# Moving parts of the second layer's vector work to GpSimd, TensorE and ScalarE in a four-layer kernel

## The chip, the cores and the metric

The kernel runs on one core of a Trainium2 chip. The metric is the device time of one execution in microseconds (us). Three runs of the kernel before took 3173.59, 3174.82 and 3178.38 us; the median is 3174.82 us.

A core has engines that work side by side, each through its own queue in order: TensorE (PE in the profile, its weight loads PEld), VectorE (DVE), ScalarE (ACT), GpSimd (POOL) and SyncE (SP), which here issues DMAs. An instruction waits for others through semaphores; while it waits, what stands behind it on its engine waits too. SBUF and PSUM are the two memories on the chip; matrix products land in PSUM.

## The reference

Four layers follow each other on x of 4 x 1024 tokens by 128 features. Each layer normalises x, makes an attention-like part s and a feed-forward part g, and adds s * silu(g) to x. The change concerns the second layer (L1):

```
xn = layernorm(x)
# attention over the 16 heads of one token (8 features each), c = 32 groups of t = 128 tokens
q, k_, v = (xn * mask) @ Wq.T + bq, ... Wk ..., ... Wv ...
scores = einsum('cthd,ctgd->cthg', q, k_) * scale      # 16 x 16 for each token
attn = entmax15(scores, axis=-1)                       # sorts each row of 16
s = einsum('cthg,ctgd->cthd', attn, v)

# feed-forward: 8 experts, the best 2 of each token, weighted
logits = x @ router_w
combine = softmax of the two largest logits, 0 elsewhere
gate = silu(einsum('th,ehf->etf', x, w1)); up = einsum('th,ehf->etf', x, w3)
out = einsum('te,eth->th', combine, einsum('etf,efh->eth', gate * up, w2))
x = x + s * silu(out)
```

The kernel puts the weight of `combine` on the input of the up product instead of the output: up is linear in x, so (c x) W3 = c (x W3).

## The kernel before, in words

Tokens lie on the 128 partitions, in 32 tiles of 128 tokens by 128 features. The second layer works in eight units of four tiles. A unit has two parts, written as generators that yield between steps: `heads1` (the attention) and `moe1` (the experts).

`heads1` first makes q, k and v of each tile with two matrix products (L729, L730) into a PSUM tile `pq`; ScalarE copies k and v to `kv` in SBUF (L731, L732). `multiply` (L716) makes the scores of one tile: a product of 16 x 16 x 8 elements for each token (L720, 2048 elements, VectorE) and a sum over the last 8 (L724, VectorE). After all four tiles it yields "scores". Then come `sort16` (L675; L698 and L699 are the maximum and minimum of pairs on VectorE, L688 and L689 copies on ScalarE, in ten stages) and the entmax on 128 x 1024 elements (L746 to L780), which goes back and forth between GpSimd (L748, L758, L759, L766, L772, L776), VectorE (two scans L752 and L753, then L761, L762, L768, L770, L771, L774) and ScalarE. Last come, for each tile, the products of attention and values (L790, GpSimd, 16 x 8 x 16 elements) and their sum over the last 16 (`values`, L785, VectorE).

`moe1` makes the logits, finds the best two (`top2`, with L197 and L198 on GpSimd) and the weights `comb` (L818). `thirds` (L204) splits `comb` into three bf16 parts (five small VectorE operations, L209 to L213) and turns them so that the tokens lie along a row (L216). `shares` (L221) spreads the row of one expert over all partitions with a bf16 product (L224). For each expert VectorE multiplies the turned input `xnT` by that row, which gives `xin` (L832); TensorE makes `pg` from `xnT` (L837) and `pu` from `xin` (L839), twice for 256 columns; ScalarE takes the silu (L840), VectorE multiplies (L841), and `down` (L828) adds the result to `po`. The down product of an expert is issued after the next expert's first products.

`layer1` (L620) runs `weave` over the present unit's heads (20 steps) and experts (11 steps), the next unit's heads up to "scores" (`upto`, 4 steps), and pieces of the third layer's preparation (`beside`). `weave` takes the part that is least far, by its share of steps. After it `update` (L648) turns the experts' result, multiplies it into s (L652, VectorE) and adds it to x (L654, GpSimd). What `weave` writes is an order of priority: when the program is built, a scheduler of the framework orders the queue of each engine by it and by the times it expects, so an operation of the next unit can stand ahead of one of this unit. Pool `p1` has one buffer of a name and `p2` two. PSUM has 4 buffers "mm", 2 "tr" and 2 "o".

Of the kernel before, what the change touches and what calls it, by code (L numbers as in the profile page):

```python
# [10 lines left out]
F32 = mybir.dt.float32  # L11
# [4 lines left out]
ALU = mybir.AluOpType  # L16
AX = mybir.AxisListType
# [3 lines left out]
P = 128  # L21
# [3 lines left out]
D = 128  # L25
# [64 lines left out]
def drain(gen):  # L90
    for _ in gen:
        pass
# [235 lines left out]
HT = NT // 2  # L328
# [291 lines left out]
def layer1(k, W, x_all, eps5, ps, beside):  # L620

    nc, tc = k.nc, k.tc
    with tc.tile_pool(name="l1", bufs=1) as p1, tc.tile_pool(name="l1d", bufs=2) as p2:

        keep = p1.tile([P, HT * 256], F32, tag="keep", name="keep")
        nc.vector.memset(keep, 1.0)
        nc.vector.memset(keep.rearrange("p (r n) -> p r n", n=16)[:, :, 0:1], 0.0)
        units = [(half, b) for half in range(2) for b in range(NB)]

        def start(half, b):  # L630
            first = b * NT + half * HT
            x = x_all[:, first : first + HT, :]
            xn = p2.tile([P, HT, D], F32, tag="xn", name="xn")
            k.layernorm(p2, x, xn, eps5, HT)
            xnT = p2.tile([P, HT * P], F32, tag="xnT", name="xnT")
            k.transpose_tiles(ps, "tr", [xn[:, t, :] for t in range(HT)], xnT)
            maskedT = None
            if half == 0:

                masked = p2.tile([P, D], F32, tag="masked", name="masked")  # L640
                nc.gpsimd.tensor_tensor(masked, xn[:, 0, :], k.c("tril"), ALU.mult)
                maskedT = p2.tile([P, P], F32, tag="maskedT", name="maskedT")
                k.transpose_tiles(ps, "tr", [masked], maskedT)
            s = p2.tile([P, HT, D], F32, tag="s", name="s")
            gT = p2.tile([P, HT * P], F32, tag="gT", name="gT")
            return x, s, gT, heads1(k, W, p1, p2, ps, xnT, maskedT, s, keep), moe1(k, W, p2, ps, xnT, gT)

        def update(x, s, gT):  # L648

            k.transpose_tiles(  # L650
                ps, "tr", [gT[:, t * P : (t + 1) * P] for t in range(HT)], s.rearrange("p t d -> p (t d)"),
                lambda out, in_: nc.vector.tensor_tensor(out, out, in_, ALU.mult),  # L652
            )
            nc.gpsimd.tensor_tensor(x, x, s, ALU.add)  # L654

        def upto(heads):

            while next(heads) != "scores":
                yield

        now = start(*units[0])
        drain(upto(now[3]))
        for n in range(len(units)):
            x, s, gT, heads, moe = now
            parts = [(heads, 20), (moe, 11)]
            if n + 1 < len(units):
                now = start(*units[n + 1])
                parts.append((upto(now[3]), 4))
                parts.append((islice(beside, 2), 2))
            weave(*parts)  # L670
            update(x, s, gT)
        drain(beside)
# [34 lines left out]
def heads1(k, W, p1, p2, ps, xnT, maskedT, s, keep):  # L707

    nc = k.nc
    R = 4 * 16  # L710
    kv = p2.tile([P, 4, 2, P], F32, tag="kv", name="kv")
    score = p2.tile([P, 4, 16, 16], F32, tag="score", name="score")

    pqs = []

    def multiply(t):  # L716

        each = [P, 16, 16, 8]
        prod = p2.tile(each, F32, tag="prods", name="prod")
        nc.vector.tensor_tensor(  # L720
            prod, pqs[t][:, 0:P].rearrange("p (h d) -> p h d", d=8).unsqueeze(2).to_broadcast(each),
            kv[:, t, 0, :].rearrange("p (g d) -> p g d", d=8).unsqueeze(1).to_broadcast(each), ALU.mult,
        )
        nc.vector.tensor_reduce(score[:, t], prod, AX.X, ALU.add)  # L724

    for t in range(4):
        lhsT = maskedT if maskedT is not None and t == 0 else xnT[:, t * P : (t + 1) * P]
        pq = ps.tile([P, 512], F32, tag="mm", name="pq")
        nc.tensor.matmul(pq[:, 0:384], lhsT, W["bd"].rearrange("p n c -> p (n c)"), start=True, stop=False)  # L729
        nc.tensor.matmul(pq[:, 0:384], k.c("ones")[0:1, :], W["bias"][0:1].rearrange("p n h d -> p (n h d)"), start=False, stop=True)  # L730
        nc.scalar.copy(kv[:, t, 0, :], pq[:, P : 2 * P])  # L731
        nc.scalar.copy(kv[:, t, 1, :].rearrange("p (d g) -> p g d", d=8), pq[:, 2 * P : 3 * P].rearrange("p (g d) -> p g d", d=8))  # L732
        pqs.append(pq)
        if t == 0:
            continue
        multiply(t - 1)
        yield
    multiply(3)
    yield "scores"
    scf = score.rearrange("p t h g -> p (t h g)")  # L740
    rows = lambda a: a.rearrange("p (r n) -> p r n", n=16)
    wide = lambda a: a.unsqueeze(2).to_broadcast([P, R, 16])
    srt = yield from sort16(k, p2, scf, R)
    new = lambda name: (p2 if name == "rest" else p1).tile([P, R * 16], F32, tag=name, name=name)
    top = p2.tile([P, R], F32, tag="top", name="top")
    nc.scalar.copy(top, rows(srt)[:, :, 0])  # L746
    z, zz, cum, rest = new("z"), new("zz"), new("cum"), new("rest")
    nc.gpsimd.tensor_tensor(rows(z), rows(srt), wide(top), ALU.subtract)  # L748
    nc.scalar.activation(zz, z, AF.Square)

    nc.gpsimd.memset(rows(zz)[:, :, 0:1], -1.0)
    nc.vector.tensor_tensor_scan(cum, keep, z, 0.0, ALU.mult, ALU.add)  # L752
    nc.vector.tensor_tensor_scan(rest, keep, zz, 0.0, ALU.mult, ALU.subtract)  # L753
    yield

    kinv = k.c("kinv").unsqueeze(1).to_broadcast([P, R, 16])
    mean, t1 = zz, cum
    nc.gpsimd.tensor_tensor(rows(mean), rows(cum), kinv, ALU.mult)  # L758
    nc.gpsimd.tensor_tensor(rows(rest), rows(rest), kinv, ALU.mult)  # L759
    nc.scalar.activation(t1, mean, AF.Square)  # L760
    nc.vector.tensor_tensor(t1, t1, rest, ALU.add)  # L761
    nc.vector.tensor_scalar(t1, t1, 0.0, None, op0=ALU.max)  # L762
    nc.scalar.activation(t1, t1, AF.Sqrt)
    yield
    tau = mean
    nc.gpsimd.tensor_tensor(tau, mean, t1, ALU.subtract)  # L766

    nc.vector.tensor_tensor(t1, tau, z, ALU.is_le)  # L768
    size = p2.tile([P, R], F32, tag="size", name="size")
    nc.vector.tensor_reduce(size, rows(t1), AX.X, ALU.add)  # L770
    nc.vector.tensor_tensor(rows(t1), k.c("kidx").unsqueeze(1).to_broadcast([P, R, 16]), wide(size), ALU.is_equal)  # L771
    nc.gpsimd.tensor_tensor(t1, t1, tau, ALU.mult)  # L772
    yield
    nc.vector.tensor_reduce(size, rows(t1), AX.X, ALU.add)  # L774
    nc.vector.tensor_tensor(size, size, top, ALU.add)
    nc.gpsimd.tensor_tensor(rows(t1), rows(scf), wide(size), ALU.subtract)  # L776
    yield
    attn = rest
    nc.scalar.activation(attn, t1, AF.Relu)
    nc.scalar.activation(attn, attn, AF.Square)  # L780
    yield
    before = None

    def values(t, prod):
        nc.vector.tensor_reduce(s[:, t, :].rearrange("p (h d) -> p h d", d=8), prod, AX.X, ALU.add)  # L785

    for t in range(4):
        each = [P, 16, 8, 16]
        prod = p2.tile(each, F32, tag="prodv", name="prod")
        nc.gpsimd.tensor_tensor(  # L790
            prod, attn.rearrange("p (t h g) -> p t h g", t=4, g=16)[:, t].unsqueeze(2).to_broadcast(each),
            kv[:, t, 1, :].rearrange("p (d g) -> p d g", d=8).unsqueeze(1).to_broadcast(each), ALU.mult,
        )
        if t:
            values(t - 1, before)
        before = prod
        yield
    values(3, before)


def moe1(k, W, p2, ps, xnT, gT):
    nc = k.nc
    pl = ps.tile([P, 512], F32, tag="o", name="pl")
    for t in range(HT):
# [7 lines left out]
    comb = p2.tile([P, HT, 8], F32, tag="comb", name="comb")  # L812
# [4 lines left out]
    nc.vector.reciprocal(best, best)  # L817
    nc.vector.tensor_tensor(comb, comb, best.unsqueeze(2).to_broadcast([P, HT, 8]), ALU.mult)  # L818

    thirds = k.thirds(p2, ps, comb, "m1")  # L820
    yield
    po = ps.tile([P, 512], F32, tag="o", name="po")
    share = k.shares(ps, thirds, 0)
    before = None

    def down(e, h):
# [1 line left out]
            nc.tensor.matmul(po, W["w2"][:, e, c, :], h[:, c, :], start=(e == 0 and c == 0), stop=(e == 7 and c == 1))  # L828

    for e in range(8):  # L830
        xin = p2.tile([P, 512], F32, tag="xin", name="xin")
        nc.vector.tensor_tensor(xin, xnT, share, ALU.mult)  # L832
        share = k.shares(ps, thirds, e + 1) if e < 7 else None
        h = p2.tile([P, 2, 512], F32, tag="h", name="h")
        for c in range(2):
            pg = ps.tile([P, 512], F32, tag="mm", name="pg")
# [4 lines left out]
            nc.vector.tensor_tensor(h[:, c, :], h[:, c, :], pu, ALU.mult)  # L841
        if before is not None:
            down(e - 1, before)
        before = h
        yield
    down(7, before)
    nc.scalar.activation(gT, po, AF.Silu)
# [1414 lines left out]
```

## Time and profile before

| what | value |
|---|---|
| median of three runs | 3174.82 us |
| the profiled execution, its own time | 3175.99 us |
| its span in the profile | 3174.2 us |
| mean granted TensorE clock | 0.738 |
| the second layer, from its first statistics to its last update | 576.3 to 1274.0 us |
| VectorE busy from 560 to 1275 us | 572.2 us |
| TensorE busy there | 517.0 us |
| GpSimd busy there | 280.7 us |
| ScalarE busy there | 247.4 us |

Busy time is the time in which an engine has an instruction under way; it says nothing about whether that instruction was the one that others waited for. In the lines of the profile, an entry of the timeline reads: start in us, duration in us, engine, line of the kernel, operation, output <- inputs, shapes, count, and in brackets the idle time of the engine before it with what ended it. Neighbouring equal entries are merged, as x4 tells. An entry of a group reads: line, engine, operation, output <- inputs, shapes, count, then busy us and mean ns of one, then idle us before them and what ended it. A line of the table by stretch reads: stretch, its length, busy us and count of PE, PEld, DVE, ACT and POOL, the granted TensorE clock as a share of full speed, the DMA share and GB/s.

### The profile page before, as it was taken

Reading aid. Unit: us, or ns where it says so; the run is one execution under the profiler, and the core shown is the slowest. Engines: PE = TensorE matmul, PEld = TensorE weight load, DVE = VectorE, ACT = ScalarE, POOL = GpSimd, SP = SyncE. Lnnn points to the kernel's source line nnn. Section 1 sums busy time; section 2 is a strip of 40 time slices with the busy share of each in tenths; the row PEclk is TensorE's granted clock in tenths of the full one; section 3 lists DMA queues with packets and bytes.
Section 4 is the critical chain, followed back from the end, with each engine's and each line's share of the span. In section 5 each row is a group of like instructions: output and inputs, shape, how many; then the busy total and the mean of one; then the engine's idle time right before and its main releaser. Section 6 shows DMA issues by size and latency. Waiting matters only on the chain. (4 is left out here: it accounts for less than half of the span.)

```text
span 3174.2 us, 47753 instructions
## 1 busy us (share of the span) xinstructions
PE 2163.6 (68%) x17039; PEld 1256.8 (40%) x17041; DVE 2291.8 (72%) x5558; ACT 1542.6 (49%) x3300; POOL 1167.5 (37%) x1094
## 2 busy tenths in 40 slices
PE   5777777577887776794543574375777777777865
PEld 2555555232332232562210122253544544544543
DVE  5554544878888786656778888676788797687777
ACT  3554544333333333535432463145765775775773
POOL 3433444144444434123477433232333332323322
PEclk9888888588888887895655566565766666766666
DMA  3000000100000000230334356339588588678772
GB/s 78 16 1 1 1 1 1 35 0 0 0 0 0 7 7 7 103 110 20 74 92 114 123 120 136 100 118 295 174 256 272 176 268 261 197 242 269 215 242 66
DMA packets 334065, 333.13 MB, mean 105 GB/s; under 512 B 25968, under 2 KB 307436, under 8 KB 328196
## 3 DMA queue, kind: packets, MB, share of 16 engines
q1 hardware_dynamic: 332676, 325.90, 34.6%
q10 hardware_dynamic: 1152, 4.19, 0.4%
q8 instruction: 134, 2.20, 0.3%
q14 instruction: 103, 0.84, 0.1%
HBM read 175.31 MB, written 154.14 MB: 104 GB/s over the span
## 5 line engine op out<-in xcount | busy, mean ns | idle before, releaser
L2120 ACT ACTIVATE neg<-neg,low 128x640 f32<-128x640 f32 (+7 forms) x512 | 390.7, 766 | 105.8 <-DVE low L2113 104.6
L1807 DVE STREAM_TRANSPOSE wT<-neg 128x640 f32<-128x640 f32 (+7 forms) x512 | 366.3, 754 | 50.3 <-PE po L2134 45.5
L2064 POOL TENSOR_SCALAR_AFFINE_SELECT rel<-rel 128x512 f32<-128x512 f32 x288 | 180.5, 638 | 551.4 <-DMA rel<-flat 412.6
L2134 PE MATMUL po<-wT,vb 128*32 128x64 f32 (+1 forms) x10240 | 266.2, 253 | 71.9 <-issue 40.8
L2097 PE MATMUL score<-k,q 32*128 32x512 f32 (+3 forms) x768 | 220.5, 587 | 124.6 <-DVE low L2113 121.3
L2134 PEld LDWEIGHTS po<-wT,vb 128*32 128x32 f32 x10240 | 210.9, 134 | 144.5 <-issue 84.1
L2113 DVE CUSTOM_DVE_ANT_0 neg<-score,rel,low 128x128 f32<-128x128 f32 (+3 forms) x448 | 213.0, 510 | 71.4 <-PE score L2097 29.3
L2035 ACT COPY r<-pr 128x512 f32<-128x512 f32 x256 | 135.2, 584 | 126.4 <-PE pr L2033 79.8
L2113 DVE CUSTOM_DVE_ANT_0 neg<-score,rel 128x512 f32<-128x512 f32 (+3 forms) x320 | 150.6, 520 | 50.4 <-POOL rel L2064 21.2
L2097 PEld LDWEIGHTS score<-k,q 32*128 32x128 f32 x768 | 96.8, 247 | 214.1 <-DVE low L2113 139.6
L837 PE MATMUL pg<-xnT,w 128*128 128x512 f32 x256 | 149.1, 666 | 7.1 <-DVE h L841 4.0
L2033 PE MATMUL pr<-emb,q 32*128 32x256 f32 x512 | 125.8, 426 | 39.7 <-ACT r L2035 25.5
L840 ACT ACTIVATE h<-pg 128x512 f32<-128x512 f32 x128 | 75.9, 596 | 157.5 <-PE pg L837 154.1
L790 POOL TENSOR_TENSOR prod<-rest,kv 128x2048 f32<-128x2048 f32 x32 | 145.5, 4598 | 18.4 <-ACT rest L780 18.4
L839 PE MATMUL pu<-xin,w 128*128 128x512 f32 x256 | 140.5, 632 | 12.9 <-DVE h L841 7.4
L828 PE MATMUL po<-h,w 128*128 128x512 f32 x256 | 129.8, 628 | 26.5 <-DVE h L841 26.5
L216 PE MATMUL pt<-ident,three 128*24 128x128 bf16 x64 | 9.2, 295 | 196.6 <-DVE three L213 196.6
L2033 PEld LDWEIGHTS pr<-emb,q 32*128 32x128 f32 x512 | 89.0, 262 | 74.4 <-ACT r L2035 38.9
L433 PE MATMUL px<-hT,xbcT 128*128 128x512 f32 x256 | 115.0, 593 | 0.0
L1086 PE MATMUL ph<-xin,upT 128*128 128x512 bf16 (+1 forms) x126 | 68.3, 572 | 66.4 <-DVE xin L1080 64.0
L1491 PE MATMUL read<-kt,const_sb 128*128 128x128 f32 x256 | 51.1, 372 | 90.3 <-POOL kt L1486 90.3
L785 DVE TENSOR_REDUCE s<-prod 128x128 f32<-128x2048 f32 x32 | 73.1, 2284 | 49.6 <-POOL prod L790 49.6
(633 smaller groups left out, 5775.7 us busy)
## 6 DMA issues: line engine op xcount, KB each, us to landing
flat<-r SPq DMA_DIRECT2D x128, 512.0 KB
rel<-flat SPq DMA_DIRECT2D x112, 512.0 KB
flat<-r SPq DMA_DIRECT2D x128, 256.0 KB
rel<-flat SPq DMA_DIRECT2D x96, 256.0 KB
kt<-kd SPq DMA_DIRECT2D x16, 512.0 KB
qt<-qd SPq DMA_DIRECT2D x16, 512.0 KB
kdc<-kdd SPq DMA_DIRECT2D x16, 512.0 KB
ktc<-ktd SPq DMA_DIRECT2D x16, 512.0 KB
```

Of the source, the lines that this page charges most:

```text
L790: nc.gpsimd.tensor_tensor(prod, attn.rearrange("p (t h g) -> p t h g", t=4, g=16)[:, t].unsqueeze(2).to_broadcast(each), kv[:, t, 1, :].re ...
L828: nc.tensor.matmul(po, W["w2"][:, e, c, :], h[:, c, :], start=(e == 0 and c == 0), stop=(e == 7 and c == 1))
L837: nc.tensor.matmul(pg, W["w1"][:, e, c * P : (c + 1) * P], xnT, start=True, stop=True)
L839: nc.tensor.matmul(pu, W["w3"][:, e, c * P : (c + 1) * P], xin, start=True, stop=True)
L1807: nc.vector.transpose(weights[at, pair][j][:, t % 2, 0 : (t + 1) * P], S[j][:, 0 : (t + 1) * P])
L2033: nc.tensor.matmul(to[:, m, :], q[at, t * P : (t + 1) * P], W["emb"][at, i, :], start=True, stop=True)
L2035: nc.scalar.copy(r[:, n], to)
L2064: nc.gpsimd.affine_select(out=rel[:, :, slot(back), :], in_=rel[:, :, slot(0), :], compare_op=op, fill=fill, base=0, pattern=[[0, 4], [-si ...
L2097: nc.tensor.matmul(halves[j // 2][:, j % 2, 0 : last - first], q[at(j), 1 + t * P : 1 + n], kk[at(j), first:last], start=True, stop=True)
L2113: nc.vector.tensor_tensor_reduce(out=neg[:, begin:last], in0=sc[:, begin - first : last - first], in1=rel[:, j, slot : slot + (last - begi ...
L2120: nc.scalar.activation(neg[:, 0:n], neg[:, 0:n], AF.Exp, bias=here, scale=-1.0, accum_out=group["sums"][:, j, t : t + 1])
L2134: nc.tensor.matmul(o[32 * j : 32 * j + 32, 2 * pair + m.start : 2 * pair + 2, :], vb[:, kb % 4 * NT + kb // 4, j].rearrange("p a d -> p (a ...
```

## The change

Three things change in the second layer.

1. The experts' inputs. `thirds`, `shares` and the VectorE product L832 go. GpSimd multiplies the normalised tokens `xn` (tokens on partitions) by the expert's column of `comb`, broadcast over 128 features (`weighted`), two experts ahead. One expert ahead, TensorE turns the four tiles into a PSUM tile "tr" and ScalarE copies it to `xin` (`turned`).
2. The sum over values. After L790 GpSimd adds the second eight of the sixteen products to the first eight, in place, and L785 sums 8 instead of 16.
3. The scores. The product of the first of four tiles moves to GpSimd, from a copy `own` of q that ScalarE makes, since the product read PSUM before. Its sum stays on VectorE and is issued after the third tile's. With this the generator yields one time less before "scores": the first step now issues three tiles' projections and the second tile's scores, the next the third tile's, and the last the first tile's sum and the fourth tile's scores.

```diff
-    def multiply(t):
+    def multiply(t, engine, q):
...
-        nc.vector.tensor_tensor(
-            prod, pqs[t][:, 0:P].rearrange("p (h d) -> p h d", d=8).unsqueeze(2).to_broadcast(each),
+        engine.tensor_tensor(
+            prod, q.rearrange("p (h d) -> p h d", d=8).unsqueeze(2).to_broadcast(each),
...
-        nc.vector.tensor_reduce(score[:, t], prod, AX.X, ALU.add)
+        return lambda: nc.vector.tensor_reduce(score[:, t], prod, AX.X, ALU.add)
...
         if t == 0:
+            own = p1.tile([P, P], F32, tag="own", name="own")
+            nc.scalar.copy(own, pq[:, 0:P])
+            slow = multiply(0, nc.gpsimd, own)
+        if t < 2:
             continue
-        multiply(t - 1)
-        yield
-    multiply(3)
+        multiply(t - 1, nc.vector, pqs[t - 1][:, 0:P])()
+        yield
+    slow()
+    multiply(3, nc.vector, pqs[3][:, 0:P])()
     yield "scores"
...
+        nc.gpsimd.tensor_tensor(prod[:, :, :, 0:8], prod[:, :, :, 0:8], prod[:, :, :, 8:16], ALU.add)
         if t:
             values(t - 1, before)
-        before = prod
+        before = prod[:, :, :, 0:8]
...
-    thirds = k.thirds(p2, ps, comb, "m1")
+    def weighted(e):
+        if e < 8:
+            xs = p2.tile([P, HT, D], F32, tag="xs", name="xs")
+            nc.gpsimd.tensor_tensor(xs, xn, comb[:, :, e].unsqueeze(2).to_broadcast([P, HT, D]), ALU.mult)
+            return xs
+
+    def turned(xs):
+        if xs is not None:
+            xin = p2.tile([P, 512], F32, tag="xin", name="xin")
+            k.transpose_tiles(ps, "tr", [xs[:, t, :] for t in range(HT)], xin, nc.scalar.copy)
+            return xin
+
+    xs = weighted(0)
     yield
     po = ps.tile([P, 512], F32, tag="o", name="po")
-    share = k.shares(ps, thirds, 0)
+    xin, xs = turned(xs), weighted(1)
...
     for e in range(8):
-        xin = p2.tile([P, 512], F32, tag="xin", name="xin")
-        nc.vector.tensor_tensor(xin, xnT, share, ALU.mult)
-        share = k.shares(ps, thirds, e + 1) if e < 7 else None
+        then, xs = turned(xs), weighted(e + 2)
...
-        before = h
+        before, xin = h, then
```

`moe1` gets `xn` as a further argument for this.

More of the change, by code (lines that the diff above doesn't have):

```diff
@@ L645, in start @@
             gT = p2.tile([P, HT * P], F32, tag="gT", name="gT")
-            return x, s, gT, heads1(k, W, p1, p2, ps, xnT, maskedT, s, keep), moe1(k, W, p2, ps, xnT, gT)
+            return x, s, gT, heads1(k, W, p1, p2, ps, xnT, maskedT, s, keep), moe1(k, W, p2, ps, xn, xnT, gT)
         def update(x, s, gT):
@@ L793, in heads1, with moe1 @@
         )
+        nc.gpsimd.tensor_tensor(prod[:, :, :, 0:8], prod[:, :, :, 0:8], prod[:, :, :, 8:16], ALU.add)
         if t:
             values(t - 1, before)
-        before = prod
+        before = prod[:, :, :, 0:8]
         yield
     values(3, before)
-def moe1(k, W, p2, ps, xnT, gT):
+def moe1(k, W, p2, ps, xn, xnT, gT):
     nc = k.nc
```

## The prediction

> **What bounds the kernel now.** The change touches one stage only, the second layer, so I first looked for it in the table of busy time by stretch of time. I cut the stretches where GpSimd adds a unit's result to `x_all` (L654): 689.1, 775.1, 860.5, 944.6, 1030.4, 1114.0, 1199.0 and 1272.8 us. Seven units thus follow each other at 86.0, 85.3, 84.1, 85.8, 83.6, 85.0 and 73.8 us; the eighth, the first in time, ends at 689.1. Two of them, and then the one from 775.14 cut at the first and the last act of its chain:
>
> ```profile
> core 0: us, PE busy (x) PEld busy (x) DVE busy (x) ACT busy (x) POOL busy (x), PEclk, DMA share, GB/s
> 774.00:858.00 84.00, 63.53 (x148) 25.46 (x148) 69.89 (x92) 29.77 (x58) 34.62 (x14) 0.82 0.00 0
> 858.00:942.00 84.00, 63.64 (x137) 25.44 (x138) 68.72 (x92) 28.34 (x53) 33.77 (x14) 0.79 0.00 0
> ```
>
> ```profile
> 775.14:802.67 27.53, 15.12 (x30) 5.67 (x30) 24.66 (x51) 10.38 (x26) 3.37 (x4) 0.55 0.00 0
> 802.67:838.52 35.85, 34.24 (x79) 12.95 (x79) 29.61 (x31) 14.75 (x23) 12.89 (x7) 1.00 0.00 0
> 838.52:860.48 21.96, 14.76 (x42) 7.32 (x41) 16.96 (x13) 4.63 (x10) 18.36 (x5) 0.87 0.00 0
> ```
>
> VectorE is busy for 70 of 84 us, GpSimd for 34: on the average there is room on GpSimd. But the limits differ by part. In the first (the sort) VectorE is full. In the second (the entmax) work goes in a ring GpSimd, VectorE, ScalarE, and TensorE is full as well (34.2 of 35.9 us). In the third (the value products) GpSimd is full. The timeline of GpSimd over this unit says in which order they stand:
>
> ```profile
> 802.67 1.93 POOL L748 TENSOR_TENSOR z<-sorted,top 128x1024 f32<-128x1024 f32 x1 [24.08 <-ACT top L746]
> 809.79 2.07 POOL L758 TENSOR_TENSOR zz<-cum,const_sb 128x1024 f32<-128x1024 f32 x1 [3.83 <-DVE rest L753]
> 811.80 2.10 POOL L759 TENSOR_TENSOR rest<-rest,const_sb 128x1024 f32<-128x1024 f32 x1
> 821.68 2.35 POOL L766 TENSOR_TENSOR zz<-zz,cum 128x1024 f32<-128x1024 f32 x1 [7.78 <-ACT cum L763]
> 829.68 2.36 POOL L772 TENSOR_TENSOR cum<-cum,zz 128x1024 f32<-128x1024 f32 x1 [5.65 <-DVE cum L771]
> 834.34 1.93 POOL L776 TENSOR_TENSOR cum<-score,size 128x1024 f32<-128x1024 f32 x1 [2.30 <-DVE size L775]
> 838.52 18.36 POOL L790 TENSOR_TENSOR prod<-rest,kv 128x2048 f32<-128x2048 f32 x4 [2.25 <-ACT rest L780]
> 860.48 1.64 POOL L654 TENSOR_TENSOR x_all<-x_all,s 128x512 f32<-128x512 f32 x1 [3.59 <-DVE s L652]
> ```
>
> The four products stand back to back, and the timeline of VectorE beside them shows who waits for whom:
>
> ```profile
> 839.76 3.83 DVE L698 TENSOR_TENSOR sorted<-score 128x512 f32<-128x512 f32 x1
> ...
> 847.99 2.29 DVE L785 TENSOR_REDUCE s<-prod 128x128 f32<-128x2048 f32 x1 [1.61 <-POOL prod L790]
> ...
> 856.92 2.29 DVE L785 TENSOR_REDUCE s<-prod 128x128 f32<-128x2048 f32 x1 [2.18 <-POOL prod L790]
> ...
> 859.72 0.68 DVE L652 TENSOR_TENSOR s<-s,pt 128x512 f32<-128x512 f32 x1
> 860.32 0.69 DVE L699 TENSOR_TENSOR sorted<-score 128x512 f32<-128x512 f32 x1
> ```
>
> VectorE waits 1.61 and 2.18 us for products. One sort operation of the next unit (L698) is drawn forward; its sister L699, and the rest of that sort, come only after the last sum and the update. So a unit's period is a chain: sort 27.5, entmax 35.9, products with the update 22.0 us. The last unit is the test: it has no next unit's four score products (18.2 us of VectorE) beside it. Its sort part shrinks to 15.6 us, almost by what VectorE lost there; its entmax takes 33.2 still. VectorE's relief pays in the sort, hardly in the entmax, and not at all in the products.
>
> **The change, part by part.** The rows of the seven units' stretch, of which all is removed, a quarter, or about a half:
>
> ```profile
> L720 DVE TENSOR_TENSOR prod<-pq,kv 128x2048 f32<-128x2048 f32 x24 | 54.8, 2284 | 5.3 <-ACT kv L732 5.3
> L724 DVE TENSOR_REDUCE score<-prod 128x256 f32<-128x2048 f32 x24 | 54.6, 2276 | 0.0
> L785 DVE TENSOR_REDUCE s<-prod 128x128 f32<-128x2048 f32 x22 | 50.2, 2284 | 29.9 <-POOL prod L790 29.9
> L832 DVE TENSOR_TENSOR xin<-xnT,pb 128x512 f32<-128x512 f32 x48 | 32.0, 678 | 0.1
> ```
>
> Per unit VectorE loses 8 x 0.68 (xin), one 2.28 (score product), 4 x 1.07 (a reduction of 1024 elements takes 1.21 at L774 instead of 2.28), and 5 x 0.17 for the thirds: 12.9 us of 70. GpSimd gains one score product of the size of L790 (4.59, from 18.36 / 4), four additions of 1024 elements (2.35 as L766, two full inputs), and eight scalings of 512 elements. The nearest rows for those are half of L748, also with a broadcast input (0.97), and L654 with two full inputs (1.27): I take 1.0, for the broadcast. Together 22.0 us: 34 becomes 56. ScalarE gains eight copies of 512 columns (0.58 each, L2035) and one small copy; at 30 of 84 us busy that hides, at most 4.9 us if each stood in the chain. TensorE loses eight L224 (0.38 warm) and gains 32 turns, which take 0.15 each warm (0.60 for four of L125 at 855.7): +1.8 us; 3.0 cold ones (0.28 each) change little.
>
> Now the chain of one unit.
>
> (a) Products. 4 x (4.59 + 2.35) = 27.8 us for 18.4: +9.4. The last reduction is 1.08 shorter. **+8.3**. Nothing hides this: GpSimd does nothing else in that part.
>
> (b) Sort. VectorE sheds the thirds (0.1 each from start to start, 0.5) and two xin (0.6 each): -1.7. The score product does not come off here: the code now makes the second and third product in the first two steps, where before it made the first and second, so two are left between the sort's operations. Against it stands what GpSimd now does beside the sort: the slow score product and about four scalings. L698 above took 3.83 us beside L790 where L699 of the same form takes 0.69 alone, and it ended 0.56 after that product did: it waited for the end. The sort is of such operations, 12 us in 27. So the slow product costs VectorE from 0 to 4.6, half: 2.3; the scalings from 0 to 4 x 1.0, half: 2.0. **+2.6**.
>
> The Trainium skill, "SBUF — State Buffer", section "Who interferes with whom", says that a VectorE operation with two SBUF inputs and a GpSimd operation that reads SBUF exclude each other for a whole instruction, and that the order of issue decides; the 3.83 us agrees. By that rule taken at its hardest, each of the five GpSimd operations of (b) would be paid in full, 8.6 instead of 4.3 us a unit, some 30 us more over the layer; by a row without a lock 30 us less.
>
> (c) Entmax. Of the xin there, four stood in front of an operation of the chain (L753, L761, L762, L770), 0.6 each: -2.4. At the half of the unit the first product's late reduction and the fourth product stand in front of L761 (6.8 us for 4.6: +2.3), for 0.2 later. The last four scalings go between GpSimd's chain operations: from 0 (it is idle for 22 of these 36 us) to 4.0; one in three meets one: 1.3. **+1.0**. A new wait comes with them: a scaling waits for TensorE to have turned the one two before it (two buffers), and L748 to L776 can be queued behind it.
>
> (d) What is drawn forward. The products' part is 30 us long with some 10 us of VectorE in it, so more of the next sort can start. Bounds: nothing, as the sister L699 above shows; or all 12 us of it. Each such operation waits for a GpSimd operation's end and then holds the next up (the product after L698 took 4.97 for 4.51, 0.46 longer): eight boundaries give 8 x 0.6 and cost 8 x 0.46. With VectorE's work of one SBUF input, which does not wait so (L785 takes its 2.27 beside a product): **-5**, nearer to the middle.
>
> Sum: 8.3 + 2.6 + 1.0 - 5 = +6.9 us a unit, 48 over seven. The first unit's preparation (four products one after another, 585.7 to 604.3) loses 2.3. In the last unit the experts end the work (its `gT` is done at 1271.2, its last sum at 1268): the 8.3 show as about +4. Net +50. The profiled execution took 3176.0 us (span 3174.2), 1.2 over the median of the runs shown; 3176 + 50 = **3226 us**.
>
> **The rivals.** *The tail is covered* (faster). If the next sort runs under the products as a whole, the period is no longer the heads' chain but the experts': from L193 at 775.2 to the end of `gT` at 855.0, 79.8 us, with 1.5 for the update. It starts 2 earlier (5.5 us from `comb` to the first expert become about 3.5) and gains 1.8: 81 us, 3.9 under the mean of the first six. Times seven: 27 off, **3149**. It decides as soon as more than 12 us of the next unit's VectorE work go under the products, (d) at -12 instead of -5. For it: VectorE idles 20 us there. Against: just one or two sort operations were drawn forward so far.
>
> *The queues lock into each other* (much slower). TensorE holds turned inputs in front of each expert's products; they wait for GpSimd, which may stand behind a 4.6 us product or the pair L758, L759 that waits for VectorE's scans (3.83 + 4.2). One such stop at half of the experts, 2 us each, adds 8 to the 6.9: +15 x 7 = 105, **3281**. For it: before, nothing on GpSimd waited for TensorE's experts. Against: a scaling is asked for two experts ahead, some 12 us.
>
> *Nothing to measure*: (d) at -12 with (b), (c) as above, **3176**.
>
> **How the numbers follow.** Forecast 0.6; covered tail 0.2; locked queues 0.13; nothing 0.07. The forecast by itself: 3195 (no lock cost) to 3260 (nothing drawn forward). The range of 8 in 10 reaches half into both outer cases: 3150 to 3285. A difference under 0.2% is about what a measurement of this kernel can't tell from no change. Faster 0.2, same 0.07, slower 0.73.
>
> **What would show it.** After: L790 with its additions should fill about 28 us without a hole, the parts 28 to 30, 36 to 37 and 30 us, VectorE 57 to 62 us busy in some 91, GpSimd 56, and sort operations of 2 to 4 us beside GpSimd's. Wrong, if the period falls though the products' part is longer: then the next sort stands inside it. Wrong in (a), if the additions take less than 2 us; in (b), if no sort operation is longer than 0.7.

## The result

After the change an execution takes 3261.24 us (median of four runs, 3253.8 to 3263.52), against 3176.6 for the kernel before in four runs beside them: the ratio is 1.0255 [1.0236, 1.0274], slower by 85 us. The forecast was 3226 in a range of 3150 to 3285. The sign and the range held; of the 85 us the sum had found 50.

### The profile after

The profiled execution took 3260.79 us (span 3259.0). The second layer ends at 1359.4 us instead of 1274.0: these 85.4 us are the whole difference (the spans differ by 84.8). New line numbers: L795 is the value product, L799 the new addition, L790 its sum, L829 the scaling, L125 the turns, L846, L853, L855 the experts' products, L856 the silu, L857 the product behind it, L753 the first operation of the entmax on GpSimd; L698 and L699 are the sort as before.

Two units in the table by stretch, from update to update:

```profile
711.40:811.90 100.50, 71.21 (x171) 31.22 (x170) 91.36 (x87) 37.78 (x75) 63.73 (x31) 0.79 0.00 0
916.90:1017.60 100.70, 65.25 (x169) 28.74 (x169) 74.98 (x81) 36.06 (x70) 59.23 (x30) 0.82 0.00 0
```

The third of the busy times is VectorE's. It had 70 us of work a unit, of which some 13 were taken away, and it is busy for 91 and 75. Where that comes from is seen in the costliest groups of the layer, first of the kernel before, then of the one after:

```profile
L698 DVE TENSOR_TENSOR sorted<-sorted 128x512 f32<-128x512 f32 (+4 forms) x88 | 47.0, 534 | 1.9 <-ACT sorted L689 0.8
L699 DVE TENSOR_TENSOR sorted<-sorted 128x512 f32<-128x512 f32 (+4 forms) x88 | 46.3, 526 | 0.0
```

```profile
L699 DVE TENSOR_TENSOR sorted<-sorted 128x512 f32<-128x512 f32 (+4 forms) x88 | 90.5, 1029 | 0.0
L698 DVE TENSOR_TENSOR sorted<-sorted 128x512 f32<-128x512 f32 (+4 forms) x88 | 88.6, 1006 | 3.6 <-ACT sorted L689 0.5 <-DVE sorted L699 0.5
L799 POOL TENSOR_TENSOR prod<-prod 128x1024 f32<-128x1024 f32 x32 | 80.6, 2534 | 0.4
```

The same sort operations, of the same shapes, take twice as long. With the first stage (L698 and L699 on `score`) all 192 of them sum to 218.5 us instead of 117.4; 46 last over 1.2 us, where it was 5. A waiting operation is recorded as a busy one here: about the 103 us that VectorE shed (8 x 12.9) came back as 101 us of waiting in the sort alone.

The timeline of GpSimd in the products of the unit that ends at 1017 shows the additions where they were expected, and that scalings stand between them:

```profile
945.62 8.99 POOL L795 TENSOR_TENSOR prod<-rest,kv 128x2048 f32<-128x2048 f32 x2 [0.59 <-ACT rest L785]
954.57 1.04 POOL L829 TENSOR_TENSOR xs<-xn,comb 128x512 f32<-128x512 f32 x1
955.58 4.62 POOL L799 TENSOR_TENSOR prod<-prod 128x1024 f32<-128x1024 f32 x2
960.17 1.04 POOL L829 TENSOR_TENSOR xs<-xn,comb 128x512 f32<-128x512 f32 x1
961.17 9.37 POOL L795 TENSOR_TENSOR prod<-rest,kv 128x2048 f32<-128x2048 f32 x2
970.50 5.49 POOL L799 TENSOR_TENSOR prod<-prod 128x1024 f32<-128x1024 f32 x2
```

VectorE from 962 us on, beside the last two products and additions:

```profile
961.96 4.23 DVE L698 TENSOR_TENSOR sorted<-score 128x512 f32<-128x512 f32 x1
966.12 0.68 DVE L857 TENSOR_TENSOR h<-h,pu 128x512 f32<-128x512 f32 x1
966.71 4.38 DVE L699 TENSOR_TENSOR sorted<-score 128x512 f32<-128x512 f32 x1
971.13 2.69 DVE L698 TENSOR_TENSOR sorted<-sorted 128x512 f32<-128x512 f32 x1
973.74 2.80 DVE L699 TENSOR_TENSOR sorted<-sorted 128x512 f32<-128x512 f32 x1
```

Each sort operation lasts until a GpSimd operation beside it has ended: the L699 of 4.38 us ends at 971.09, behind the second product at 970.54, and the last L699 at 976.54, behind the second addition at 975.99. Alone such an operation takes 0.69. Read on to what stands behind it. L857, the product that an expert waits for, has just one input in SBUF and takes 0.68, but stands in VectorE's queue behind an L698 of 4.23. And ScalarE and TensorE at that time:

```profile
976.58 0.71 ACT L688 COPY sorted<-sorted 128x256 f32<-128x256 f32 x1 [16.59 <-DVE sorted L699]
...
977.68 1.12 ACT L856 ACTIVATE h<-pg 128x512 f32<-128x512 f32 x2
```

```profile
966.85 1.12 PE L855 MATMUL pu<-xin,w 128*128 128x512 f32 x2 [2.76 <-DVE h L857]
...
978.37 2.08 PE L853 MATMUL pg<-xnT,w 128*128 128x512 f32 x2 [8.24 <-ACT h L856]
```

ScalarE's queue holds the next unit's sort copies (L688, L689) ahead of this unit's silu. ScalarE stands idle for 16.59 us, until sort operations that wait for GpSimd let the copies go; the silu waits behind them, and TensorE stops for 8.24 us for want of a PSUM buffer that the silu would free. The last sum of this unit ends at 978.8, but the experts' `gT` only at 1011.1. In six of eight units the experts now end last, by 21 to 39 us; before, the heads ended last in six.

So I cut the layer along the experts' path, at the end of `comb`, the end of `gT` and the update. The parts add up to the whole:

| us, all eight units | before | after | difference |
|---|---|---|---|
| up to the first `comb` | 621.0 | 624.2 | +3.2 |
| `comb` to `gT` | 513.1 | 605.2 | +92.1 |
| `gT` to the update's end | 45.5 | 47.0 | +1.5 |
| update to the next `comb` | 94.4 | 83.0 | -11.4 |
| end of the layer | 1274.0 | 1359.4 | +85.4 |

The loss lies between `comb` and `gT`. TensorE's idle time ahead of the experts' three products there went from 46.5 us (7.1, 12.9, 26.5) to 112.3 (37.1, 43.5, 31.7), nearly all of it put down to the silu and to L857. The three groups before, then after:

```profile
L837 PE MATMUL pg<-xnT,w 128*128 128x512 f32 x256 | 149.1, 666 | 7.1 <-DVE h L841 4.0 <-ACT h L840 2.3 <-DVE xin L832 0.5
L839 PE MATMUL pu<-xin,w 128*128 128x512 f32 x256 | 140.5, 632 | 12.9 <-DVE h L841 7.4 <-DVE xin L832 2.8 <-DVE prod L720 2.6
L828 PE MATMUL po<-h,w 128*128 128x512 f32 x256 | 129.8, 628 | 26.5 <-DVE h L841 26.5
```

```profile
L853 PE MATMUL pg<-xnT,w 128*128 128x512 f32 x256 | 148.6, 665 | 37.1 <-ACT h L856 28.5 <-DVE h L857 8.4
L855 PE MATMUL pu<-xin,w 128*128 128x512 f32 x256 | 151.2, 676 | 43.5 <-DVE h L857 41.0 <-ACT h L856 2.0 <-ACT xin L126 0.2
L846 PE MATMUL po<-h,w 128*128 128x512 f32 x256 | 136.3, 659 | 31.7 <-DVE h L857 31.5
```

### The profile page after: what moved, and what is told of

It reads as the page before. It is cut to its first block, busy times and chain, and to the rows that moved or that the text cites. A ratio compares the mean times of both kernels' runs of the same rounds, so it can differ in the third digit from the quotient of the medians.

```text
span 3259.0 us, 48169 instructions
## 1 busy us (share of the span) xinstructions
PE 2204.4 (68%) x17201; PEld 1297.5 (40%) x17201; DVE 2323.4 (71%) x5442; ACT 1579.6 (48%) x3374; POOL 1356.4 (42%) x1198
## 5 line engine op out<-in xcount | busy, mean ns | idle before, releaser
L855 PE MATMUL pu<-xin,w 128*128 128x512 f32 x256 | 151.2, 676 | 43.5 <-DVE h L857 41.0
L853 PE MATMUL pg<-xnT,w 128*128 128x512 f32 x256 | 148.6, 665 | 37.1 <-ACT h L856 28.5
L846 PE MATMUL po<-h,w 128*128 128x512 f32 x256 | 136.3, 659 | 31.7 <-DVE h L857 31.5
L795 POOL TENSOR_TENSOR prod<-rest,kv 128x2048 f32<-128x2048 f32 x32 | 146.3, 4587 | 15.5 <-DVE s L790 8.3
L857 DVE TENSOR_TENSOR h<-h,pu 128x512 f32<-128x512 f32 x128 | 86.0, 679 | 50.7 <-PE pu L855 42.6
L829 POOL TENSOR_TENSOR xs<-xn,comb 128x512 f32<-128x512 f32 x64 | 73.4, 1157 | 81.8 <-PE pt L125 37.1
L125 PE MATMUL pt<-const_sb,xs 128*128 128x128 f32 x256 | 45.9, 313 | 84.1 <-POOL xs L829 68.3
```

Of the source, the lines that this page charges most:

```text
L795: nc.gpsimd.tensor_tensor(prod, attn.rearrange("p (t h g) -> p t h g", t=4, g=16)[:, t].unsqueeze(2).to_broadcast(each), kv[:, t, 1, :].re ...
L853: nc.tensor.matmul(pg, W["w1"][:, e, c * P : (c + 1) * P], xnT, start=True, stop=True)
L855: nc.tensor.matmul(pu, W["w3"][:, e, c * P : (c + 1) * P], xin, start=True, stop=True)
```

## The experiments

Theory of the lock: a GpSimd operation that reads SBUF holds up VectorE's operations of two SBUF inputs for its whole length; the wait falls on them and on all that stands behind them in the queues. Rivals: GpSimd is simply too long now; the scalings' path GpSimd, TensorE, ScalarE is too slow for the experts; the drawing forward itself does harm. Sort sum below means the durations of the 192 sort operations in the layer (before 117.4, after 218.5).

### One part at a time

The first run makes just the scaled inputs (part 1), the second just the additions (part 2), the third just the score product (part 3). Each is the kernel after with the other two parts as they were before:

```diff
     # part 1
-    share = k.shares(ps, thirds, 0)
+    xin, xs = turned(xs), weighted(1)
...
-        nc.vector.tensor_tensor(xin, xnT, share, ALU.mult)
+        then, xs = turned(xs), weighted(e + 2)
     # part 2
+        nc.gpsimd.tensor_tensor(prod[:, :, :, 0:8], prod[:, :, :, 0:8], prod[:, :, :, 8:16], ALU.add)
...
-        before = prod
+        before = prod[:, :, :, 0:8]
     # part 3
+            nc.scalar.copy(own, pq[:, 0:P])
+            slow = multiply(0, nc.gpsimd, own)
...
+    slow()
```

> Part 1 of the change alone (GpSimd scales the tokens, TensorE turns them, ScalarE copies); sums and scores as before. Theory 'lock' (VectorE operations with two SBUF inputs wait for the whole of a GpSimd operation, and the experts' L841 and comb wait behind them in VectorE's queue): the scalings are 1 us each, so little is held up, 3160 to 3195 us. Theory 'length' (GpSimd's longer products' part lengthens the heads' chain): unchanged products, 3165 to 3185. Theory 'feed' (the experts wait for scaled and turned inputs): most of the 85 us, 3220 to 3260.

> Part 2 alone (GpSimd adds the two halves after each value product, VectorE sums 8 instead of 16). Lock: next unit's sort operations drawn under a GpSimd part that is 9 us longer, each taking 2 to 4 us, with L841 behind them: 3195 to 3230. Length: the heads' chain is 8.3 longer in eight units, 3235 to 3245, and no VectorE operation needs to be longer for it. Feed: VectorE is relieved and nothing else, 3150 to 3177.

> Part 3 alone (the first tile's score product on GpSimd, its sum issued late). Lock: sort operations and the small operations that make comb stand behind a 4.5 us product once a unit, so comb comes later by 3 to 5 us: 3185 to 3215. Length and feed: VectorE loses 2.3 us a unit where it is full, 3155 to 3177.

| run | us | ratio to before | sort sum | GpSimd, sum of durations from 560 us to the layer's end |
|---|---|---|---|---|
| before | 3176 | 1 | 117.4 | 283 |
| part 1 | 3185.35 | 1.0026 [1.0012, 1.004] | 172.5 | 366 |
| part 2 | 3248.72 | 1.0219 [1.0199, 1.0239] | 217.6 | 367 |
| part 3 | 3217.38 | 1.013 [1.0114, 1.0146] | 190.2 | 320 |
| all | 3261.24 | 1.0255 [1.0236, 1.0274] | 218.5 | 476 |

Each part loses by itself; by the differences of medians 9, 72 and 41 us, together more than the 85 of the whole. The path over TensorE and ScalarE is all in part 1, which costs 9 us net, what it spares VectorE counted in: as the cause of the 85 that rival falls. Part 2 gives GpSimd as much more as part 1 (84 and 83 us) and costs eight times as much: it puts them into the part of the unit where GpSimd was already full. Part 3 gives it just 37 more, for 41.

Against the expectations: part 1 lies in the lock's range and at the upper end of the length's, far from the feed's. Part 2 lies 19 us above the lock's range and 4 above the length's, yet its sort operations grew to 217.6 us, as the lock says and the length does not ask for: this run doesn't decide between the two. Part 3 lies 2 above the lock's range and 40 above the other's.

### GpSimd's products in pieces

If the length of one GpSimd operation is what a VectorE operation waits for, shorter ones should cost less. The whole change, with four products of 512 elements for one of 2048, and two additions for one:

```diff
-        nc.gpsimd.tensor_tensor(prod, ...)
+        for h in range(0, 16, 4):
+            nc.gpsimd.tensor_tensor(prod[:, h : h + 4], ...)
```

> The whole change, but GpSimd's score product and value products in four pieces of 512 elements and the additions in two pieces, so that none lasts over about 1.3 us. The computation is the same. Lock: a VectorE operation now waits 1.3 us at most instead of 4.5; the waiting sort operations shrink from 2.7 to 4.4 us to under 2, and the time falls to 3190 to 3225. Length and feed: the same work or a little more, 3260 to 3285.

3288.88 us, ratio 1.0352 [1.0337, 1.0368]: worse than the whole change, 64 us above what the lock was to give and 4 above the range of length and feed. The sort sum fell to 190.6, and all sort operations but two now take under 3 us. But GpSimd takes longer: the value products 168.7 us together instead of 146.3, and VectorE's sums waited 118.9 us for GpSimd instead of 49.8. More than half of the 22 us is the price of small operations: the shortest piece takes 1.24 us, four of them 4.96, and the shortest whole product 4.47. The rest would be GpSimd's own waiting.

The two other sort operations are the larger surprise. They took 9.10 and 16.36 us. The second of them, the stop of TensorE behind it, and GpSimd at that time:

```profile
1053.40 16.36 DVE L698 TENSOR_TENSOR sorted<-score 128x512 f32<-128x512 f32 x1
```

```profile
1072.87 2.07 PE L861 MATMUL pu<-xin,w 128*128 128x512 f32 x2 [13.50 <-DVE h L863]
```

```profile
1052.61 4.90 POOL L800 TENSOR_TENSOR prod<-rest,kv 128x512 f32<-128x512 f32 x4
1057.47 2.46 POOL L805 TENSOR_TENSOR prod<-prod 128x512 f32<-128x512 f32 x2
1059.90 3.67 POOL L800 TENSOR_TENSOR prod<-rest,kv 128x512 f32<-128x512 f32 x3
1063.54 1.04 POOL L835 TENSOR_TENSOR xs<-xn,comb 128x512 f32<-128x512 f32 x1
1064.54 1.24 POOL L800 TENSOR_TENSOR prod<-rest,kv 128x512 f32<-128x512 f32 x1
1065.75 2.45 POOL L805 TENSOR_TENSOR prod<-prod 128x512 f32<-128x512 f32 x2
1068.17 1.04 POOL L835 TENSOR_TENSOR xs<-xn,comb 128x512 f32<-128x512 f32 x1
```

Fourteen GpSimd operations stand back to back, and the sort operation ends only behind the last of them: a waiting VectorE operation doesn't always get in when the GpSimd operation beside it ends. So the expectation's "1.3 us at most" was wrong. Why these two were passed over, and the others not, no run here shows.

### GpSimd without the reads

Next the load was kept and the reading taken away. Value products and additions become a tiny product (which keeps the order) and memory sets, which just write. What is left out: the products over values and GpSimd's additions, so s isn't the reference's; VectorE's sums stay and read what the sets wrote.

```diff
-        nc.gpsimd.tensor_tensor(prod, attn..., kv..., ALU.mult)
-        nc.gpsimd.tensor_tensor(prod[:, :, :, 0:8], prod[:, :, :, 0:8], prod[:, :, :, 8:16], ALU.add)
+        nc.gpsimd.tensor_tensor(prod[:, :, 0, 0], <16 elements of attn>, <16 of kv>, ALU.mult)
+        nc.gpsimd.memset(prod, 0.5)
+        nc.gpsimd.memset(prod, 0.5)
+        nc.gpsimd.memset(prod[:, :, :, 0:8], 0.5)
```

> The whole change, but each value product and its addition on GpSimd are replaced by a product of 16 elements a token (which keeps the wait for attn) and memsets of 2048, 2048 and 1024 elements: GpSimd is still occupied for some microseconds a tile, but reads next to nothing from SBUF there. The sums over values are left out, so s is not the reference's. Lock: the sort operations drawn under that part fall from 2.3 to 4.4 us back to 0.7, the experts' products are no longer held up, and the time falls to 3170 to 3215 us. Length: if the memsets last as long as the products and additions did (6.9 us a tile), 3245 to 3265; if they are shorter, 8 x 4 x the difference less.

3141.14 us, 0.9892 [0.987, 0.9914], 29 us below the lock's range; sort sum 121.3. But a set of 2048 elements took 1.81 us, so that a tile took 4.8 us of GpSimd rather than 6.9: length and reading had changed together. The next run evens that out with one more set of 2048 and one of 256 (7.1 us a tile):

> As e5_no_reads, with one more memset of 2048 and one of 256 elements a tile, so that GpSimd is occupied for about 7.0 us a tile as by the product and the addition (6.94 us); again the sums over values are left out. e5's GpSimd was 2.2 us a tile shorter, 69 us over the layer. Lock: only the reading costs, so most of the 120 us that e5 gained over the whole change stays, 3150 to 3200 us, with sort operations of 0.7 us. Length: the time goes back to 3245 to 3265 us.

3150.35 us, 0.9899 [0.9878, 0.9919]. GpSimd is as busy as in the kernel after (474.5 against 475.5 us) and the loss of 85 us has become a gain of 28. The time lies at the lower edge of the lock's range and 95 us below the length's. Length costs at most the 9 us between the medians of these two runs, whose intervals overlap. The counterpart is to exclude that the gain came from shorter instructions or from their number: the same instructions, of the same sizes, as copies that read.

```diff
-        nc.gpsimd.memset(prod, 0.5)
+        nc.gpsimd.tensor_copy(prod, <kv, broadcast>)
```

> The counterpart of the run with memory sets of equal length: the same whole change, the same number and the same sizes of GpSimd instructions, but each memory set (2048, 2048, 2048, 1024 and 256 elements) becomes a GpSimd copy of the same size from the values in SBUF. Left out, as there: the value products and the additions, so s isn't the reference's. Only one thing differs from that run: these instructions read SBUF. Theory of the lock: the sort's operations and the other VectorE operations wait again, the sort's sum goes from 128 back to 170 to 220 us and the time from 3150 to 3220 to 3270. Rival (the gain there came from the shorter instructions, from their number or from another order of the queues, not from the missing reads): 3140 to 3170, sort sum under 140. No profile here has a GpSimd copy of this size; should one take much longer or shorter than the set's 1.81 us, the difference in length counts at the small rate that the two runs with sets gave, 9 us for 2.3 us a tile.

3232.92 us, 1.0159 [1.0142, 1.0176], in the lock's range; sort sum 220.5. The groups of the run with sets and of the run with copies:

```profile
L800 POOL MEMSET prod<- 128x2048 f32 x32 | 57.6, 1805 | 0.1
...
L698 DVE TENSOR_TENSOR sorted<-sorted 128x512 f32<-128x512 f32 (+4 forms) x88 | 56.5, 642 | 4.5 <-ACT sorted L689 2.2
```

```profile
L800 POOL COPY prod<-kv 128x2048 f32<-128x2048 f32 (+2 forms) x160 | 250.9, 1612 | 0.6
L698 DVE TENSOR_TENSOR sorted<-sorted 128x512 f32<-128x512 f32 (+4 forms) x88 | 105.0, 1193 | 3.1 <-ACT sorted L689 0.4
```

One edit, from writing to reading, doubles the sort operations and costs 83 us. The group of the copies mixes their three sizes; those of 2048 elements take 2.14 us on the mean for the 1.81 of a set, with waits in them. GpSimd is busy 50 us longer over the layer; at the rate of the two runs with sets (9 us for 2.3 us a tile) these 1.6 us a tile are worth 6, an estimate. The rival of length falls, that of the number of instructions too. The loss goes another way here, though: the heads end 26 us after `gT` in seven of the eight units, since their copies alternate with the sort's operations (46 us for the products' part), while in the kernel after it is the experts that end late. The framework's scheduler orders the queues anew for each kernel (a few hundred of VectorE's 5442 instructions stand elsewhere in these two), so a few us of any of these differences may be order.

### The next sort held back

Does the drawing forward harm, since it puts the sort beside GpSimd's products? The whole change, with the next unit's first sort stage (p == 1) queued behind the update's L652, which is kept as `k.gate`:

```diff
-            for pair in pairs:
...
+            behind = getattr(k, "gate", None) if p == 1 else None
+            with k.tc.issue_after(behind.ins) if behind is not None else nullcontext():
+                for pair in pairs:
...
```

> The whole change, with the first stage of the next unit's sort queued on VectorE behind this unit's update, so that no sort operation stands under the value products. Queue theory (the sort operations that wait for GpSimd hold up the experts' products behind them, and that makes most of the loss): the experts take 55 to 60 us again and the time falls to 3195 to 3235. Chain theory (the prediction's: sort, entmax and longer products now follow one another without overlap, +11.9 us a unit): 3255 to 3275.

3283.37 us, 1.0335 [1.0311, 1.0359]: 22 worse than with the drawing forward, so it is still a gain. The queue theory's range is missed by 48 us, the chain theory's by 8. The sort sum is 133.2. The kernel has become a chain again: in the unit that ends at 998.5 the sort takes 37.1 us, the entmax 32.2, the products 28.2 (as in each of the eight units), and with the update the period is 98.8; the other periods are 96 to 102 us, the last 82.

### Part 1 without GpSimd, and what drawing forward is worth

Three runs for a version that keeps what part 1 takes from VectorE. The scaling on ScalarE, with the other parts as before:

```diff
-            nc.gpsimd.tensor_tensor(xs, xn, comb[:, :, e].unsqueeze(2).to_broadcast([P, HT, D]), ALU.mult)
+            for t in range(HT):
+                nc.scalar.activation(xs[:, t, :], xn[:, t, :], AF.Identity, scale=comb[:, t, e : e + 1])
```

> Part 1 alone, but the scaling is done by ScalarE (four activations of 128x128 an expert with the weight as their scale) instead of GpSimd: VectorE sheds the same 6.6 us a unit, and GpSimd gets nothing, so no sort operation waits longer. Lock: the 55 us that the sort operations gained with part 1 on GpSimd are gone, 3125 to 3165 us. If it is the feed of the experts or ScalarE's queue that costs (15.4 us more a unit on ScalarE): 3180 to 3220.

3185.88 us, 1.0029 [1.0015, 1.0044], as with GpSimd: 21 us above the lock's range, and in the one for the feed or ScalarE's queue. GpSimd has not one instruction more than before, and the sort sum still goes from 117.4 to 157.8, since more of the next sort stands under the old value products: beside those the sort operations take 42 us more than the shortest of their shapes, for 13 before. Whether that or ScalarE's queue takes back what VectorE was spared, this run doesn't show. Then both forms of part 1 with the next sort held back as above:

> Scaling on ScalarE as in e7 and the next unit's sort queued behind the update as in e6; value sums and scores as in the kernel before. In e7 the sort operations took 158 us instead of 117, although GpSimd had no more to do: VectorE's free time was filled with sort operations under the value products, where they wait. Lock: held back, they return to some 118 us, each unit saves about 3.5 us of chain, 3140 to 3170 us. If something else costs in e7 (ScalarE's queue, the feed of the experts): 3180 to 3200.

> Scaling on GpSimd as in e1, with the next unit's sort queued behind the update. Lock: as e9, but the scalings themselves still meet the sort (2 us a unit): 3155 to 3185 us. Otherwise about e1's 3185 or more.

3212.16 us, 1.0094 [1.0073, 1.0115], and 3197.21, 1.0058 [1.0037, 1.008]. What the lock was to give was missed both times: though the sort sums fell to 110.0 and 131.0, the time rose, by 26 and 12 us. The first lies even above the range for another cause (3200), the second where it was expected without the lock ("3185 or more"). So in three kernels out of three a drawn-forward sort that waits in the lock is better than one that comes later, though in the third pair the intervals just overlap. What costs the version on ScalarE its 34 us over the kernel before isn't found: the holding back, ScalarE's queue and the place of the next unit's scores (three products and three sums stand between the sort's operations, for two and two before) are all left. None of these versions beats the kernel before.

## Why the prediction was right in sign and short in size

By units, the sum had +4.6 for the first (6.9 - 2.3), 6.9 for each of the next six and +4 for the last. Measured at the updates: +21.0, 11.6 on the mean (69.4 in all), and -5.1. That the sum found as much as 50 of the 85 us is in part luck: it adds up the heads' chain, and in six of eight units it isn't that chain that ends last.

- **(a) Products, +8.3: right in itself.** Where the next sort does not interfere, the part takes 28.2 us in each unit (the held run) up to the end of the last sum, for 20.2 to 20.7 before; 4 x (4.59 + 2.35) and the last sum gave 29.0; additions took 2.33 there. In the kernel after it is no block without a hole, as I had said it would be: scalings stand between, and it takes 31.7 to 36.8.
- **(b) Sort, +2.6: the mechanism right, the size far short.** I priced 4.3 us a unit of waiting, for five GpSimd operations at half their length each. The sort operations alone wait 101 / 8 = 12.6 us a unit, mostly not for those five but for value products and additions. A second reading was wrong too: I had said that two score products would be left between the sort's operations. In the first unit and in six of the first seven of the held run three products and four sums stand there, for two and two before, 6.8 us more; the held run's sort part, 37.1 us for 27.5, grew by 9.6 where I had 2.6. The rule of the Trainium skill that I had weighed there ("SBUF — State Buffer", section "Who interferes with whom") speaks of reads, and also says that a GpSimd operation that only writes does not contend. The pair of runs with sets and copies agrees: sort sum 128 beside writes, 220 beside reads. Even its hardest form in the prediction, 30 us more over the layer, came to 80, 5 under the measured 85, but for waits in another place than those it counted.
- **(c) Entmax, +1.0**: the held run's 32.2 for 35.9 before shows no loss there; in the kernel after it can't be told apart, since it overlaps the unit before.
- **(d) Drawn forward, -5: this is the step that failed.** The bounds were nothing and all 12 us of the sort; in six of seven cases it was all: L753 of the next unit starts at 994.4, for example, before the update at 1016.3. That was the condition that I had set for the rival "the tail is covered": the experts' chain then sets the period. It does. But I had let that chain shorten, from the 79.8 us of before, because I counted what the drawn-forward operations cost GpSimd (0.46 each) and not what they cost whoever stands behind them. From L193 at 915.5 to `gT` at 1011.1 it takes 95.6. In this unit `comb` comes 7 later after L193 than before (23.4 for 16.3), and the last silu 13 later after `comb` (66.2 for 53.2): L857 behind sort operations of 4 us, the silu behind L688.
- **First unit**: I took its -2.3 from the start of the preparation. Its sort part grew from 24.6 to 34.8, for more of the next unit's score products had been drawn into it (seven products and sums of 2.3 us for four), and its products' part from 20.4 to 33.1.
- **The rival "the queues lock into each other"** had the right word and the wrong place: the stops of the experts come mostly not from scalings queued on GpSimd (15 us of TensorE's idle time between `comb` and `gT` are put down to them) but from sort operations queued on VectorE and ScalarE.

What stays open is a part of the 92 us between `comb` and `gT`. TensorE's idle time in these stretches, summed over the rows of both traces, grew by 65, from 79 to 144. Ahead of the experts' products it grew by 66; ahead of what makes `xin` it stayed the same, 31.1 us at the turns for 32.5 at the turns and spreads of the thirds (L216, L224), so that late inputs add nothing to it. In the other 27 us TensorE has work; they are not assigned.

## What to carry to other kernels

An engine with idle time is a place for work only if the work doesn't take a path that another engine needs at that moment. In this kernel that was so where a GpSimd operation read SBUF beside a VectorE operation of two SBUF inputs: look for such pairs, and find them in the profile as a group whose mean duration doubles at unchanged shape. A wait that is recorded as busy time also hides in the share of busy time, so compare the mean durations of unchanged operations and not the busy shares. And when work is drawn forward into a gap, price not only what it does to its own chain but what then stands behind it on each queue that it passes.

## What the runs showed of the hardware that was not expected

The timelines of VectorE and of GpSimd at the start of the same unit:

```profile
919.67 4.11 DVE L819 TENSOR_TENSOR comb<-logit,best 128x32 f32<-128x32 f32 x1
923.71 2.37 DVE L201 TENSOR_SCALAR two<-rank 128x32 f32<-128x32 f32 x1
```

```profile
919.26 4.47 POOL L720 TENSOR_TENSOR prod<-own,kv 128x2048 f32<-128x2048 f32 x1
923.70 2.34 POOL L777 TENSOR_TENSOR cum<-cum,zz 128x1024 f32<-128x1024 f32 x1
```

- The price doesn't go by the size of the operation that waits. L819 takes 0.18 us alone and 4.11 here, since it ends with GpSimd's L720; an L698 of 16 times as many elements took 4.23 beside a product.
- L201 waits too (2.37 us for 0.17), though it has just one input in SBUF; the reductions of 2048 elements, also of one input, take 2.27 to 2.29 us beside GpSimd's products and alone. The same section of the Trainium skill names `tensor_scalar` among the operations that can enter a mode with two ports, and `tensor_reduce` as one that can't; these rows agree.
- Pieces made it worse, not better: products of 512 elements took 1.35 us each and 168.7 together, for 146.3 in whole products, and one sort operation stood through fourteen GpSimd operations (16.36 us).
- A GpSimd memory set of 2048 f32 took 1.81 us, and of the 31 sort operations of 512 elements that ran for the greater part beside sets of 1024 or 2048, 29 took 0.68 to 0.69.
